# Second part's q from a natural-order table, three list segments, pinned scatters and later lists in a sparse attention kernel

## The chip, the cores and the metric

The kernel runs on one core of a Trainium2 chip. The engines named here are PE (TensorE, matrix products, with its weight loads shown as PEld), DVE (VectorE), ACT (ScalarE), POOL (GpSimd, which here mostly issues indirect DMAs) and SP (SyncE, which issues plain DMAs). The metric is the device time of one execution in microseconds (us). Three runs of the kernel before took 1813.91, 1814.09 and 1817.4 us, a median of 1814.09.

## The reference

One graph attention layer over N = 4096 nodes with D = 512 features and H = 8 heads of 64, all in float32. The adjacency matrix is 4096 x 4096 int32 and sparse: a node has about 17 neighbours, itself among them.

```python
hs = layer_norm(x, ln1_scale, ln1_bias)
ht = layer_norm(h_target, ln1_scale, ln1_bias)
q = (ht @ Wq + bq).reshape(T, H, HD) / sqrt(HD)
k = (hs @ Wk + bk).reshape(S, H, HD)
v = (hs @ Wv + bv).reshape(S, H, HD)
logits = einsum('thd,shd->hts', q, k)
logits = where(adj != 0, logits, -1e30)
ctx = einsum('hts,shd->thd', softmax(logits), v).reshape(T, D)
ht = layer_norm(ht + ctx @ Wo + bo, ln2_scale, ln2_bias)
y = ht + gelu(ht @ W1) @ W2
out = layernorm(x + y)
```

## The kernel before

**Lists instead of a dense matrix.** The kernel builds, for every node (a row), the list of its neighbours, and then works only on these. A row of adjacency is read in four quarters of 1024 columns. ACT turns a quarter into bytes of 0 and 1 (L729), DVE reads two bytes as one 16-bit word, multiplies it by a number that grows with the position (L734, `lio`), and takes the eight largest words of each of SQ = 5 segments of a quarter (L736). From these 20 x 8 words it splits the low and the high byte (L743, L744), adds the offset of the segment (L748, L751), and picks the 24 largest of 320 numbers in three rounds (L755, L757). All 320 numbers of a row also go to DRAM (`rest_d`, L767) for the few rows with more neighbours. A check that the counts agree guards this. If it fails, a slow general path runs.

**Two parts, sorted.** Rows 0 to 2047 are the first part and rows 2048 to 4095 the second. Within a part, `sort` (L808) ranks the rows by their number of neighbours on DVE and PE, and 16 indirect DMAs of POOL (L854) scatter the records of the rows (count, row number, normalisation, list) into rank order in DRAM. 128 rows of like length make a tile, and a tile is worked through with as many slots as its longest row needs: 302 slots for the first 16 tiles (tile 0 to 15, with 11 slots at first, up to 39) and 301 for tiles 16 to 31.

**Stages.** First the projections: for each block of 256 rows of x, normalise, transpose, make k and v, and write them to a DRAM table `kvd` (L936). Beside them the lists of the first part, and of the first five blocks of the second, are made. Then attention runs tile by tile over all 32 tiles. `prefetch` (L971) loads a tile's record with a DMA of POOL's queue (L980). `front` (L983) makes q: it gathers the tile's rows of h_target (POOL), scales them (L999, ACT), transposes them (L1003, PE), applies the first layer norm's scale and bias (L1006, ACT), multiplies by Wq (L1012, PE), and scales and adds the bias (L1017, DVE). The normalised rows stay transposed in the other half of `tq`. For each slot of the tile, POOL gathers 128 rows of 4 KB from `kvd` into a ring of buffers (L1076 calls the gather, which the profile shows at L967). Three slots make a step: DVE multiplies k by q (L1220) and sums over each head (L1225), ACT takes the exponential, DVE multiplies v of two slots by it (L1184) and ACT that of the third (`by_scalar`, L1204), and PE sums the slots by transposing them into PSUM (L1192). In the second part DVE first adds two slots (L1188), which saves PE a third of that. `finish` (L1078) masks, normalises, transposes the residual back by PE (L1112), multiplies by Wo (L1116), copies the sum out (L1121, ACT), and normalises again. `feed` (L1310) is the feed-forward of a group of one or two tiles (L1325 and L1334 on PE).

**What sets the order.** The program is written as generators, each of which yields a virtual cost. `_weave` (L400) always continues the one with the least virtual time. Attention and feed-forward take 60 units for a group of two tiles. `other_lists`, the remaining 11 blocks of lists and then `sort(1)`, starts at WAIT = 40 units and takes 18 units for a block. When the program is built, each engine's instructions are put in a fixed order from this program order and from when they should be ready. `tc.issue_after(ins)` puts what is written inside it behind `ins` on that engine. Every engine then runs its instructions in that order, and an instruction that waits holds up those behind it. Buffers have names and a number of copies (`bufs`): `xt`, `gt`, `h2T`, and `t` and `pf` in PSUM have two each, and a third user waits until one is free.

## Time and profile before

| | |
|---|---|
| median of three runs | 1814.09 us |
| profiled execution | 1817.49 us |
| its span, first to last instruction | 1815.5 us |
| mean granted clock of TensorE | 0.967 |
| busy: PE, DVE, ACT, POOL | 1677.8, 1436.5, 1224.1, 982.2 us |
| share of the span | 92%, 79%, 67%, 54% |
| DMA | 463.26 MB, mean 255 GB/s |
| gathers of kvd rows | 603, of 1257 ns each on POOL |

The profile is of one execution. A row of groups gives line, engine, operation, output and inputs with their shapes and the number of instructions, then busy time and mean ns of one, and at the end the idle time of the engine just before them with what ended it. A slice table gives the busy share of each engine in tenths over 40 equal slices. A wait row says which instruction waited for which, with the total, the number of times and the longest. A busy PE is not PE at its peak, since matmuls are pipelined and their ends are modelled, and POOL's times don't include the time to issue. A float32 product of 512 columns is two instructions in the trace.

### The profile page before, as it was taken

What the parts mean: (1) busy time and instruction counts of PE and PEld (TensorE: products, weight loads), DVE (VectorE), ACT (ScalarE), POOL (GpSimd) and SP (SyncE); (2) the same over time, 40 slices, a digit from 0 to 9 for tenths busy, and PEclk for the clock granted to TensorE, in tenths of its full rate; (3) what the DMA queues carried; (4) which work ended last, traced back from release to release, by engine and by line L of the source; (5) the groups of instructions that cost most, each with busy time, mean ns of one, the idle gap of its engine ahead of it and who ended that gap; (6) DMA issues with size and microseconds to landing.
All of it is one profiled execution on the core that took longest, in us unless ns stands there. A gap on an engine that the chain in (4) does not pass through costs nothing. (4 is left out here: it accounts for less than half of the span.)

```text
span 1815.5 us, 22973 instructions
## 1 busy us (share of the span) xinstructions
PE 1677.8 (92%) x7030; PEld 1097.9 (60%) x7030; DVE 1436.5 (79%) x2660; ACT 1224.1 (67%) x3121; POOL 982.2 (54%) x834
## 2 busy tenths in 40 slices
PE   7989984597999979999999989999999999999997
PEld 3434442465766656766776757666666666666664
DVE  6989876899999837777978989978878797988200
ACT  5767654487987736766778868877777676787311
POOL 1000144656566676766678788867575665763101
PEclk9999996698999989999999999999999999999998
DMA  9999968989887557777878878787776776774000
GB/s 344 366 380 372 344 198 319 404 287 332 271 305 256 201 173 243 258 255 267 273 263 302 293 260 295 249 285 250 241 266 222 248 251 238 244 248 153 18 6 26
DMA packets 140269, 463.26 MB, mean 255 GB/s; under 512 B 16500, under 2 KB 21672, under 8 KB 140136
## 3 DMA queue, kind: packets, MB, share of 16 engines
q0 software_dynamic: 96656, 342.64, 55.8%
q1 hardware_dynamic: 35664, 95.98, 15.0%
q10 hardware_dynamic: 7816, 23.08, 3.3%
q8 instruction: 58, 0.95, 0.2%
q14 instruction: 75, 0.61, 0.1%
HBM read 430.75 MB, written 30.89 MB: 254 GB/s over the span
## 5 line engine op out<-in xcount | busy, mean ns | idle before, releaser
L967 POOL DMA_INDIRECT kv<-kvd,rec x603 | 758.1, 1257 | 347.5 <-PE cps L1192 139.7
L1334 PE MATMUL po<-w,gt 128*128 128x512 f32 x1024 | 466.4, 598 | 16.2 <-ACT gt L1328 16.2
L1325 PE MATMUL pf<-h2T,w 128*128 128x256 f32 (+1 forms) x2176 | 465.9, 368 | 0.1
L1325 PEld LDWEIGHTS pf<-h2T,w 128*128 128x128 f32 x2176 | 389.3, 191 | 64.5 <-issue 20.3
L1220 DVE TENSOR_TENSOR kv<-kv,tq 128x1536 f32<-128x1536 f32 (+2 forms) x211 | 351.6, 1675 | 68.3 <-DMA kv<-kvd,rec 56.2
L1204 ACT ACTIVATE kv<-kv,pa 128x64 f32<-128x64 f32 x1520 | 391.0, 336 | 4.3
L1225 DVE TENSOR_REDUCE lg<-kv 128x24 f32<-128x1536 f32 (+2 forms) x211 | 350.1, 1666 | 1.4
L1334 PEld LDWEIGHTS po<-w,gt 128*128 128x128 f32 x1024 | 188.8, 192 | 212.4 <-issue 194.3
L1192 PEld LDWEIGHTS cps<-ident,kv 128*128 128x128 f32 x2008 | 240.2, 145 | 109.4 <-issue 59.2
L1192 PE MATMUL cps<-ident,kv 128*128 128x128 f32 x2008 | 264.5, 280 | 44.1 <-DVE kv L1184 24.5
L1184 DVE TENSOR_TENSOR kv<-kv,p 128x1024 f32<-128x1024 f32 (+1 forms) x211 | 251.0, 1193 | 22.8 <-ACT p L1229 20.3
L687 POOL TENSOR_TENSOR n_rs<-n_ve,mhalf 128x2 f32<-128x2 f32 (+2 forms) x51 | 50.8, 997 | 329.1 <-DVE n_ve L680 165.3
L729 ACT ACTIVATE kv<-kv 128x1024 uint8<-128x1024 int32 x128 | 134.9, 1056 | 100.0 <-DMA kv<-in_adj_dram 51.7
L1328 ACT ACTIVATE gt<-pf 128x512 f32<-128x512 f32 x128 | 76.4, 597 | 93.8 <-PE pf L1325 75.8
L1328 ACT ACT_TABLE_LOAD x104 | 133.4, 1283 | 1.7
L736 DVE MAX8 cand<-kv 128x8 uint16<-128x103 uint16 (+1 forms) x640 | 131.8, 252 | 0.8 <-DVE R L755 0.2
L930 PE MATMUL pq<-wk,h2T 128*128 128x512 f32 x256 | 120.8, 616 | 12.1 <-ACT tq L932 7.2
L1012 PE MATMUL t<-wq,tq 128*128 128x512 f32 x256 | 118.2, 605 | 5.6 <-ACT tq L1006 5.6
L930 PE MATMUL pq<-wv,h2T 128*128 128x512 f32 x256 | 115.5, 594 | 6.4 <-ACT kv L729 3.0
L1229 ACT ACTIVATE p<-lg 128x24 f32<-128x24 f32 (+2 forms) x179 | 39.2, 219 | 113.0 <-DVE lg L1225 88.8
L1116 PE MATMUL t<-wo,rb 128*128 128x512 f32 x256 | 115.2, 592 | 0.0
L930 PEld LDWEIGHTS pq<-wk,h2T 128*128 128x128 f32 x256 | 48.9, 197 | 69.9 <-issue 55.2
(160 smaller groups left out, 1582.2 us busy)
## 6 DMA issues: line engine op xcount, KB each, us to landing
kv<-in_adj_dram SPq DMA_DIRECT2D x128, 512.0 KB
kvd<-tq ACTq DMA_DIRECT2D x24, 512.0 KB
kv<-kvd,rec POOLq DMA_INDIRECT x603
kv<-in_L_gnn_h_target_dram SPq DMA_DIRECT2D x32, 256.0 KB
kv<-in_x_dram SPq DMA_DIRECT2D x15, 512.0 KB
rest_d<-gid SPq DMA_DIRECT2D x32, 160.0 KB
w<-in_L_gnn_W_dram SPq DMA_DIRECT2D x4, 1024.0 KB
kvd<-kv ACTq DMA_DIRECT2D x8, 512.0 KB
```

Source lines behind the costliest of these rows:

```text
L729: nc.scalar.activation(sg, a, AF.Sign, accum_out=dpart[:, i, h:h + 1])
L736: nc.vector.max(cand[:, h * SQ + s, :], wd[:, w0:w1])
L930: nc.tensor.matmul(pkv, hT[:, kc, j * P:(j + 1) * P], w[:, kc, :], start=kc == 0, stop=kc == KC - 1)
L967: nc.gpsimd.indirect_dma_start(out=dst, out_offset=None, in_=table[:, :], in_offset=bass.IndirectOffsetOnAxis(ap=idx, axis=0))
L1184: nc.vector.tensor_tensor(v4, v4, p[:, j0:j0 + m, :].unsqueeze(3) .to_broadcast([P, m, H, HD]), ALU.mult)
L1192: nc.tensor.matmul(cps[:, c, :], kv[:, j, D + c * P:D + (c + 1) * P], ident, is_transpose=True, start=j0 + j == 0 and c == 0, stop=j0 + n ...
L1204: newest[:] = [nc.scalar.mul(v, v, pa[:, hd:hd + 1]).ins]
L1220: nc.vector.tensor_tensor(kv[:, :n, :D], kv[:, :n, :D], tq[:, :D].unsqueeze(1).to_broadcast([P, n, D]), ALU.mult)
L1225: nc.vector.tensor_reduce(lg[:, :n, :], kv[:, :n, :D].rearrange("p j (h d) -> p j h d", h=H), AX.X, ALU.add)
L1325: nc.tensor.matmul(pf[:, k, :], w1[(f0 + k) // KC][:, kc, (f0 + k) % KC * P:((f0 + k) % KC + 1) * P], h2T[:, kc, :w], start=kc == 0, stop= ...
L1328: nc.scalar.activation(gt, pf, AF.Gelu_apprx_tanh)
L1334: nc.tensor.matmul(po[j], gt[:, k, j * P:(j + 1) * P], w2[(f0 + k) // KC][:, (f0 + k) % KC, :], start=False, stop=f0 + k == FC - 1, skip_g ...
```

## The change

There are five edits.

1. A new generator, `natural`, makes q of the second part's 16 blocks of rows in natural order and writes a table `qd` in DRAM with a row of 4 KB for each node: q, and beside it the normalised row with its bias, not transposed. It is woven in with 5 units a block, from virtual time 0 on. `front` of a tile of the second part then only gathers its rows of `qd`. `finish` of such a tile leaves out the transposes of the residual, and DVE adds it in place of the copy by ACT.
2. SQ goes from 5 to 3. A segment then has up to 171 words. The position numbers grow by 1 in place of 2, so that they still fit a byte, and the sum of offset and number is made with a factor of 2 in place of the plain addition.
3. For tiles 0 to 2 (LEAN = 3) the third slot is multiplied by DVE with the other two, and `by_scalar` isn't called.
4. The scatters of the records are put behind the gather issued last, in program order (`behind(issues)`). The record of a tile of the second part is loaded by SP's queue in place of POOL's. The copy of its tags is put behind the last sum of logits.
5. WAIT goes from 40 to 80: `other_lists` starts later.

```diff
@@ -1,4 +1,4 @@
-from contextlib import ExitStack
+from contextlib import ExitStack, nullcontext
 
 import concourse.bass as bass
 import concourse.tile as tile
@@ -488,7 +488,7 @@
     NQ = 4
     QW = N // NQ
     WQ = QW // 2
-    SQ = 5
+    SQ = 3
     WS = -(-WQ // SQ)
     SEGS = [(s * WS, min(s * WS + WS, WQ)) for s in range(SQ)]
     SEG = NQ * SQ
@@ -512,6 +512,7 @@
     kvd = dram.tile([N + P, 2 * D], F32, name="kvd")
     recs_d = [dram.tile([n * P, RW], I32, name=f"rec{i}") for i, (_, n) in enumerate(PARTS)]
 
+    qd = dram.tile([NBT * P, 2 * D], F32, name="qd")
     rest_d = dram.tile([N, 2 * SEG * 8], F32, name="rest_d")
 
     flag = const.tile([1, 1], I32, name="flag")
@@ -608,12 +609,12 @@
 
             def list_constants():
                 io = turn_of("wide", wide)
-                nc.gpsimd.iota(io[:, :SQ * WS], pattern=[[0, SQ], [2, WS]], base=1,
+                nc.gpsimd.iota(io[:, :SQ * WS], pattern=[[0, SQ], [1, WS]], base=1,
                                channel_multiplier=0)
 
                 nc.vector.tensor_copy(lio, io[:, :WQ])
                 io = turn_of("wide", wide)
-                nc.gpsimd.iota(io[:, :2 * SEG], pattern=[[1, 2], [QW, NQ], [2 * WS, SQ]], base=0,
+                nc.gpsimd.iota(io[:, :2 * SEG], pattern=[[1, 2], [QW, NQ], [2 * WS, SQ]], base=-1,
                                channel_multiplier=0)
                 nc.gpsimd.iota(io[:, 2 * SEG:2 * SEG + NB], pattern=[[1, NB]], base=0,
                                channel_multiplier=0)
@@ -713,6 +714,9 @@
                     a = turn_of("wide", wide)
                 nc.sync.dma_start(a, adj[i * P:(i + 1) * P, h * QW:(h + 1) * QW])
                 return a
+
+            def behind(ins):
+                return tc.issue_after(ins[-1]) if ins else nullcontext()
 
             def edges(i):
 
@@ -748,7 +752,7 @@
                 nc.vector.scalar_tensor_tensor(gid, dec, 0.0,
                                                off.unsqueeze(2).to_broadcast([P, 2 * SEG, 8]),
                                                op0=ALU.is_gt, op1=ALU.mult)
-                nc.vector.tensor_add(gid, gid, dec)
+                nc.vector.scalar_tensor_tensor(gid, dec, 2.0, gid, op0=ALU.mult, op1=ALU.add)
                 flat = gid.rearrange("p s e -> p (s e)")
                 for r in range(RE // 8):
                     top = rec[:, E0 + r * 8:E0 + (r + 1) * 8]
@@ -851,10 +855,11 @@
                 nc.vector.tensor_copy(ranki, rank)
                 yield 10.0
                 for i in range(n):
-                    ins = nc.gpsimd.indirect_dma_start(
-                        out=recs_d[part][:, :],
-                        out_offset=bass.IndirectOffsetOnAxis(ap=ranki[:, i:i + 1], axis=0),
-                        in_=R[:, i, :], in_offset=None)
+                    with behind(issues):
+                        ins = nc.gpsimd.indirect_dma_start(
+                            out=recs_d[part][:, :],
+                            out_offset=bass.IndirectOffsetOnAxis(ap=ranki[:, i:i + 1], axis=0),
+                            in_=R[:, i, :], in_offset=None)
 
                     tc.declare_no_dep(ins.ins, group=f"scatter{part}", reason="other rows")
                     tc.add_to_no_dep_group(f"scatter{part}", ins.ins)
@@ -962,11 +967,12 @@
 
 
             recs, tqs, h2Ts, done, ready, latest, newest = {}, {}, {}, set(), [], [], []
+            issues, logits = [], []
 
             def gather(dst, table, idx):
-                nc.gpsimd.indirect_dma_start(
+                issues[:] = [nc.gpsimd.indirect_dma_start(
                     out=dst, out_offset=None, in_=table[:, :],
-                    in_offset=bass.IndirectOffsetOnAxis(ap=idx, axis=0))
+                    in_offset=bass.IndirectOffsetOnAxis(ap=idx, axis=0)).ins]
 
             def prefetch(i):
                 if i >= NT or i in recs:
@@ -977,7 +983,7 @@
                 r0 -= PARTS[part][0] * P
                 rec = sp.tile([P, E0 + MAXE], I32, name="rec", bufs=6)
 
-                nc.gpsimd.dma_start(rec[:, :RW], recs_d[part][r0:r0 + P, :])
+                (nc.sync if part else nc.gpsimd).dma_start(rec[:, :RW], recs_d[part][r0:r0 + P, :])
                 recs[i] = rec
 
             def front(i, idle=0):
@@ -985,6 +991,14 @@
 
                 rec = recs[i]
                 tq = sp.tile([P, 2 * D], F32, name="tq", bufs=3)
+                if TILES[i][0] >= PARTS[1][0] * P:
+                    gather(tq, qd, rec[:, ROW:ROW + 1])
+                    for _ in range(3 + idle):
+                        yield
+                    with behind(logits):
+                        nc.vector.tensor_copy(tags[:, i, :], rec[:, DEG:TGT + 1])
+                    tqs[i] = tq
+                    return
                 t = tq[:, :D]
                 gather(t, h_target, rec[:, TGT:TGT + 1])
                 for _ in range(1 + idle):
@@ -1108,17 +1122,22 @@
                 yield
                 pa = ps.tile([P, D], F32, name="t", bufs=2)
 
+                natural_q = TILES[i][0] >= PARTS[1][0] * P
+                if not natural_q:
+                    for c in range(KC):
+                        nc.tensor.matmul(pa[:, c * P:(c + 1) * P], tq[:, D + c * P:D + (c + 1) * P],
+                                         ident, is_transpose=True, start=c == 0, stop=False,
+                                         skip_group_check=True)
                 for c in range(KC):
-                    nc.tensor.matmul(pa[:, c * P:(c + 1) * P], tq[:, D + c * P:D + (c + 1) * P],
-                                     ident, is_transpose=True, start=c == 0, stop=False,
-                                     skip_group_check=True)
-                for c in range(KC):
-                    nc.tensor.matmul(pa, ct[:, c, :], wo[:, c, :], start=False,
+                    nc.tensor.matmul(pa, ct[:, c, :], wo[:, c, :], start=natural_q and c == 0,
                                      stop=c == KC - 1, skip_group_check=True)
                 turned.add(i)
                 yield
                 h = sp.tile([P, D], F32, name="h")
-                nc.scalar.copy(h, pa)
+                if natural_q:
+                    nc.vector.tensor_add(h, pa, tq[:, D:])
+                else:
+                    nc.scalar.copy(h, pa)
                 yield
                 stats(sp, h, mv[:, len(hs), :], "n2")
                 hs.append(h)
@@ -1179,7 +1198,7 @@
 
 
 
-                    m = n - 1 if n == S else n
+                    m = n - 1 if n == S and i >= LEAN else n
                     v4 = kv[:, :m, D:].rearrange("p j (h d) -> p j h d", h=H)
                     nc.vector.tensor_tensor(v4, v4, p[:, j0:j0 + m, :].unsqueeze(3)
                                             .to_broadcast([P, m, H, HD]), ALU.mult)
@@ -1222,9 +1241,9 @@
                                                     ALU.mult)
                             lg = sp.tile([P, S, H], F32, name="lg")
                             latest[:] = [lg[:, 0, 0:1]]
-                            nc.vector.tensor_reduce(lg[:, :n, :],
-                                                    kv[:, :n, :D].rearrange("p j (h d) -> p j h d", h=H),
-                                                    AX.X, ALU.add)
+                            logits[:] = [nc.vector.tensor_reduce(
+                                lg[:, :n, :], kv[:, :n, :D].rearrange("p j (h d) -> p j h d", h=H),
+                                AX.X, ALU.add).ins]
                             if j0 > 0:
                                 nc.scalar.activation(p[:, j0:j0 + n, :], lg[:, :n, :], AF.Exp)
                             advance()
@@ -1236,7 +1255,7 @@
                             if j0 == 0:
                                 p = sp.tile([P, MAXE, H], F32, name="p", bufs=1)
                                 nc.scalar.activation(p[:, :n, :], lg[:, :n, :], AF.Exp)
-                            if n == S:
+                            if n == S and i >= LEAN:
                                 by_scalar(kv, lg)
                             last = j0 + n == TILES[i][1]
                             after = finish(i, p, cps, group, hs, mv) if last else None
@@ -1373,11 +1392,66 @@
                                                    op0=ALU.bypass, op1=ALU.max)
 
 
+            def natural():
+
+                Rf = Rs[1].bitcast(F32)
+                ht, hTs = {}, {}
+
+                def load(b):
+                    if b < NBT:
+                        ht[b] = sp.tile([P, D], F32, name="xt")
+                        r0 = (PARTS[1][0] + b) * P
+                        nc.sync.dma_start(ht[b], h_target[r0:r0 + P, :])
+
+                def norm(b):
+                    if b < NBT:
+                        nc.scalar.activation(ht[b], ht[b], AF.Identity,
+                                             bias=Rf[:, b, RST + 1:RST + 2],
+                                             scale=Rf[:, b, RST:RST + 1])
+
+                def turn(b):
+                    t = ht.pop(b)
+                    pt = ps.tile([P, KC, P], F32, name="t", bufs=2)
+                    for kc in range(KC):
+                        nc.tensor.transpose(pt[:, kc, :], t[:, kc * P:(kc + 1) * P], ident)
+                    hT = sp.tile([P, KC, P], F32, name="gt")
+                    for kc in range(KC):
+                        nc.scalar.activation(hT[:, kc, :], pt[:, kc, :], AF.Identity,
+                                             bias=b1r[:, kc:kc + 1], scale=s1c[:, kc:kc + 1])
+                    hTs[b] = hT
+
+                def make(b):
+                    hT = hTs.pop(b)
+                    pq = psf.tile([P, D], F32, name="pf")
+                    for kc in range(KC):
+                        nc.tensor.matmul(pq, hT[:, kc, :], wq[:, kc, :], start=kc == 0,
+                                         stop=kc == KC - 1)
+                    pb = psf.tile([P, D], F32, name="pf")
+                    for kc in range(KC):
+                        nc.tensor.transpose(pb[:, kc * P:(kc + 1) * P], hT[:, kc, :], ident)
+                    qn = sp.tile([P, 2 * D], F32, name="h2T")
+                    nc.vector.scalar_tensor_tensor(qn[:, :D], pq, HD ** -0.5, bqr,
+                                                   op0=ALU.mult, op1=ALU.add)
+                    nc.scalar.copy(qn[:, D:], pb)
+                    nc.sync.dma_start(qd[b * P:(b + 1) * P, :], qn)
+
+                load(0)
+                load(1)
+                norm(0)
+                for b in range(NBT):
+                    turn(b)
+                    load(b + 2)
+                    norm(b + 1)
+                    yield 2.5
+                    make(b)
+                    yield 2.5
+
             def chain(gens):
                 for g in gens:
                     yield from g
 
-            WAIT = 40.0
+            WAIT = 80.0
+            LEAN = 3
             AHEAD = 4
             UNIT = 60.0
 
@@ -1448,7 +1522,7 @@
                 yield from sort(1)
 
             _weave((att, 0), (chain(feed(g) for g in range(len(GROUPS))), 0), (other_lists(), WAIT),
-                   (weights(), 0))
+                   (natural(), 0), (weights(), 0))
 
     left = nc.values_load(flag[0:1, 0:1], min_val=0, max_val=1)
     with tc.If(left != 0):
```

## The prediction

> **What bounds the kernel now.** The chain that ended last covers only the final 3 us, so it says nothing. I read the slices of the page first, to see the stages (a slice is 45.4 us).
>
> ```profile
> PE   7989984597999979999999989999999999999997
> DVE  6989876899999837777978989978878797988200
> PEclk9999996698999989999999999999999999999998
> DMA  9999968989887557777878878787776776774000
> ```
>
> PE is full almost everywhere. It isn't in slices 7 and 8, where the projections end and attention begins: the clock is low there too, and DMA is full. DVE has one hole, at slice 15. Next, stages, cut at the starts of the last list-edge masking of each tile (L1083: tile 2 ends at 387, tile 7 at 585, tile 8 at 631, tile 9 at 695, tile 15 at 1013, tile 31 at 1681). After the clock times come PE, PE's weight loads, DVE, ACT, POOL, then granted clock and DMA.
>
> ```profile
> 0.00:296.00 296.00, 255.46 (x675) 118.59 (x676) 246.20 (x1060) 190.68 (x354) 44.47 (x62) 0.97 0.92 330
> 296.00:387.00 91.00, 54.54 (x266) 40.48 (x265) 76.09 (x105) 48.82 (x153) 63.12 (x52) 0.74 0.95 358
> 387.00:631.00 244.00, 231.47 (x1076) 160.94 (x1075) 233.49 (x487) 194.31 (x495) 144.07 (x120) 0.97 0.81 280
> 631.00:695.00 64.00, 54.05 (x242) 37.42 (x241) 32.89 (x33) 32.73 (x89) 46.92 (x42) 0.92 0.57 197
> 695.00:1013.00 318.00, 308.83 (x1445) 216.32 (x1444) 255.40 (x263) 231.61 (x644) 226.53 (x185) 0.99 0.79 265
> 1013.00:1681.00 668.00, 651.87 (x2818) 442.60 (x2817) 579.94 (x644) 500.64 (x1348) 445.82 (x362) 0.99 0.74 248
> 1681.00:1816.00 135.00, 121.56 (x515) 81.59 (x513) 12.53 (x73) 25.33 (x46) 11.29 (x13) 0.96 0.05 17
> ```
>
> So PE bounds 695 to the end (97 to 98%), PE and DVE together bound 387 to 631 (95 and 96%), and 296 to 387 is a start with PE idle for 36.5 us of 91 and running at 0.74 of its clock. The second part (tiles 16 to 31) is the 668 us stage. Its groups on PE that make q:
>
> ```profile
> L1012 PE MATMUL t<-wq,tq 128*128 128x512 f32 x122 | 55.4, 596 | 4.9 <-ACT tq L1006 4.9
> L1112 PE MATMUL t<-ident,tq 128*128 128x128 f32 x60 | 9.0, 273 | 0.0
> L1003 PE MATMUL t<-ident,tq 128*128 128x128 f32 x60 | 9.0, 272 | 0.0
> ```
>
> and the waits of that stage which belong to q and to the ring:
>
> ```profile
> POOL kv L967 <- PE cps L1192: 54.0, 36, 8.4
> ...
> DVE tq L1017 <- PE t L1012: 24.2, 5, 6.2
> ```
>
> Last, the hole at 631, in order of time on POOL and DVE. Nine scatters of the second part's records run back to back from 627; gathers behind them come late, and DVE waits 9.4 us for one.
>
> ```profile
> 627.06 1.01 POOL L854 DMA_INDIRECT rec<-R,kv  x1 [1.53 <-DVE kv L851]
> ...
> 638.89 0.96 POOL L854 DMA_INDIRECT rec<-R,kv  x1 [0.30 <-issue]
> 640.16 0.97 POOL L967 DMA_INDIRECT kv<-kvd,rec  x1 [0.30 <-issue]
> ```
> ```profile
> 664.35 1.76 DVE L1220 TENSOR_TENSOR kv<-kv,tq 128x1536 f32<-128x1536 f32 x1 [9.37 <-DMA kv<-kvd,rec]
> ```
>
> **What the Trainium skill says.** "TensorE: Matmul & The Clock Gate", Part 1: an idle PE falls to half its clock and needs sustained work to get it back. The trace agrees: clock 0.62 between 310 and 360. "DMA: Bandwidth & Descriptors", Issuing engines are not separate DMA queues: transfers of all issuers share 16 engines. It agrees: 405 GB/s at share 1.03 in those 50 us, with gathers, weights and adjacency together. "VectorE: DVE Perf Modes", Mode 1×: one element a cycle at 0.96 GHz. MAX8 agrees: (478 - 253) ns over (320 - 103) elements is 1.04 ns each. "ScalarE: Activation LUTs", Table sets: copy and identity are in every set, so the new scalings need no table load; the group L1006 (Identity) indeed shows none.
>
> **The change, part by part.** The sum is against the profiled execution: 1817.5 us, of which 1815.5 are the span; it is 3.4 over the median 1814.1, and I subtract from the median at the end.
>
> 1. *q of the second part moved to the start (natural).* Removed from each of its tiles: PE 73.4 us over 15 tiles (the three rows above), 4.9 each; ACT 0.81 + 4 x 0.37 + 0.57 (L999, L1006, L1121) = 2.9; DVE 0.68 (L1017) + 0.22 (L995), while the residual add costs 0.68 (like L1104), so DVE is about even. Added to virtual time 0 to 80, which is tiles 0 to 2, the 296 to 387 stage: 16 x (4 transposes 0.60, 8 matmuls 3.60, 4 transposes 0.60 = 4.8, as those rows run in order of time) = 77 us of PE; ACT 16 x 2.9 = 46; DVE 16 x 0.68 = 11; SP 16 loads and 16 stores. Bytes: 16 x (0.25 read + 0.5 written) = 12 MB, at 405 GB/s 30 us of transfer, put beside gathers of 0.5 MB each; what the lists no longer load there, about 3 MB, comes off. PE's spare in that stage is 36.5 idle plus about 13 of the 54.5 busy (clock 0.74 with full-rate work after 370): 49. So 77 - 49 = 28 us of extra length; transfers alone would ask for (12 - 3)/0.405 = 22 less the 4 that the share leaves free, so they agree. Bounds: +10 (q work starts before 296, in the 25 us that PE idles from 260 to 296) and +110 (the clogged rival below).
> 2. *Second-part stage with 73 us less PE.* PE 652 - 73 = 579. But DVE keeps 577, and POOL 446 plus about 0.3 us of issue for each of 362 instructions = 555, less 16 record loads of 0.6 + 0.3 that go to SP's queue, 541. SP issues nothing else there, so these cost nothing; if SP were held up, a tile's record would be late, and POOL's gathers with it. A gather of q is 512 KB for 256: 4 MB over 600 us, hidden under a DMA share of 0.74. If PE stayed at 97.6% the stage would be 593 (-75). Two engines as closely loaded as DVE and PE now become stood at 95 to 96% from 387 to 631; with a third near I take 94%: 579/0.94 = 616, that is -52. Bounds -75 and -15. DVE's 24 us behind L1017 vanish in it; DVE next waits for POOL's power or for the ring.
> 3. *Three segments.* Five MAX8 in a row take 0.93, 0.186 each; three of 171 words take 3 x (0.186 + 68 x 1.04 ns) = 0.77: -0.16 x 4. Seven operations on 192 in place of 320 columns: -0.133 x 7. Together -1.6 us of DVE a tile; by group means -2.1. Before 296, 21 tiles: -33 to -44, but PE (255 of 296) and DMA bound that stage. Its tail, 247 to 290, has PE waiting for copies that stand behind Sign activations on ACT, which wait for adjacency and sign buffers (5 or 6 of ACT's waits, 15 + 7 us). I take -6, bounds -15 and 0.
> 4. *Lists later (WAIT 80).* About nine us of lists leave the start (DVE 76 + 11 - 9 there) and fall into 387 to 631, where DVE is at 96%: 10.5 tiles at 7.8 for 7.75 at 9.4 is +9 of DVE. I take +8, bounds 0 and +15. The records are asked for at virtual 405; the scatters now end at 346 in place of 306, so they are still 60 units, some 65 us, early.
> 5. *Scatters pinned.* Each of the 16 (1.27 us of POOL) goes behind the gather last issued, one in 3 units, so no nine in a row. The tile that took 64.3 us should take what its neighbours take, 45 to 48, plus some: -14, bounds -18 and 0. What waits behind a scatter now is one gather, not nine scatters' worth.
> 6. *Third slot by VectorE in tiles 0 to 2.* 11 full segments: DVE +11 x (1.75 - 1.21) = +6, ACT -11 x 2.2 = -24. Hidden both ways (DVE 84 of 119, ACT 49 + 46 - 24 = 71 of 119). Without that cover it costs DVE's 6.
>
> Sum: +28 - 52 - 6 + 8 - 14 = -36; 1817.5 - 36 = 1781.5, and 1778 by the median.
>
> **Rivals.** *A, PE was not what bound the second part.* POOL's 86 us behind the ring (54 for cps, 33 for L1188) and DVE's 87% stay; the stage gives back 15 to 25 instead of 52. For it: three engines would all be above 90%. Against: DVE and PE ran at 96 and 95% together before. Time: -36 + 35 = -1 to -10, so 1804 to 1813; centre 1807. *B, slower: natural clogs the start.* It shares two buffers each of xt, gt, h2T, t and pf with attention and the feed-forward. If a tile of it runs as one chain (load, 0.8, 0.6, 1.5, 3.6, 0.7, write, with load and write under a full DMA some 5 us together), 12 us each and 16 x 12 = 192 us from 290, attention's PE and ACT instructions stand behind it in order and tile 2 ends at 482: +95 in place of +28, so -36 + 67 = +31, 1845. It decides from 28 + 36 = +64: tile 2 ending after 451, about 10 us a tile. For it: DMA is full just there. Against: the loads run two ahead, and PE needs 4.8. *C, no faster lists or a lost list:* in the reference's inputs no third of a quarter row holds more than eight words with an edge, so the fallback isn't taken; I give it nothing. *D, the scatters behind gathers that wait for the ring move the hole instead of filling it:* -14 falls away, 1792; it lies in the forecast's range.
>
> **How the numbers follow.** Forecast with D: 0.56, own range 1740 to 1800. A: 0.20. B: 0.20. Something not listed: 0.04. No change that a measurement of this kernel can tell from nothing is 0.2%, 3.6 us. A's upper end gives 0.05 to "same"; B and 0.02 more are slower, 0.22; the rest is faster, 0.73. The range takes in A and half of B: 1738 to 1838.
>
> **What would show it.** Step 1: between 296 and 420 PE full at clock near 1, tile 2 ending near 415. Step 2: the last sixteen tiles in about 616 us, PE and DVE both near 94%, no wait of DVE for q. Step 3: three MAX8 of about 324 ns a quarter row. Steps 4 and 5: scatters apart by 3 us or more, no tile near 64 us, DVE full until about tile 9. The prediction is wrong if tile 2 ends after 451 (B), or if the last sixteen tiles still take 645 us (A).

## The result, and the profile after

The changed kernel is slower. Its median is 1913.0 us (four runs, 1902.88 to 1914.93) beside 1814.38 for the kernel before on the same chip: a ratio of 1.0525, 95% interval 1.049 to 1.056. (The ratios are estimates from several runs of both kernels and need not equal the quotient of two medians, here 1.0543.) The forecast was 1778, range 1738 to 1838. The profiled execution is the shortest of the four, 1902.88 us with a span of 1901.2 us, so the stages below account for 85 us over the profiled execution before, of the 99 between the medians.

The slices of the changed kernel's page (47.5 us each):

```profile
PE   7999977888798989998999998989899988989995
DVE  6898755687887667767697898989798877768200
PEclk9999989899898999999999999989899999999998
DMA  9999889877875757567787897888888776674000
```

Slices 7 and 8 of PE, a 4 and a 5 before, are a 7 and an 8, and its clock is up in them, as forecast. But DVE, which stood at 9 in slices 9 to 13 of before, is at 6 to 8 from slice 9 to 20, and PE is less often at 9 in the second half.

The stages, cut at the same tile ends as before (the masking, L1083 before, is L1097 now: tile 2 ends at 420, tile 8 at 708, tile 9 at 761, tile 15 at 1098, tile 31 at 1762; what follows tile 31 is called the tail). After the times come PE, PE's weight loads, DVE, ACT, POOL, the granted clock, and DMA's share and rate:

```profile
0.00:296.00 296.00, 262.94 (x693) 122.40 (x693) 221.23 (x876) 192.59 (x359) 50.74 (x70) 0.97 0.94 341
296.00:420.00 124.00, 100.78 (x387) 57.04 (x388) 90.08 (x127) 59.60 (x137) 47.94 (x40) 0.89 0.86 316
420.00:708.00 288.00, 255.59 (x1168) 175.39 (x1167) 221.42 (x402) 188.83 (x492) 138.34 (x121) 0.93 0.70 239
708.00:761.00 53.00, 50.82 (x240) 36.03 (x239) 36.94 (x39) 35.59 (x98) 30.50 (x28) 1.00 0.69 238
761.00:1098.00 337.00, 318.46 (x1486) 221.35 (x1485) 260.19 (x268) 231.48 (x639) 239.07 (x199) 0.99 0.75 254
1098.00:1762.00 664.00, 608.40 (x2577) 418.36 (x2575) 567.85 (x623) 470.73 (x1260) 447.02 (x349) 0.95 0.75 253
1762.00:1901.00 139.00, 117.42 (x489) 77.78 (x487) 14.17 (x76) 24.91 (x45) 11.29 (x13) 0.94 0.05 16
```

Stage by stage, before to after: 296 to tile 2's end 91 to 124 (+33), tiles 3 to 8 244 to 288 (+44), tile 9 64 to 53 (-11), tiles 10 to 15 318 to 337 (+19), the last sixteen tiles 668 to 664 (-4), the tail 135 to 139 (+4). Two things stand out. Up to the end of tile 2 the loss is about as forecast (the end was expected near 415 and came at 420), but tiles 3 to 8 then lose another 44 us, where 8 were forecast. And the last sixteen tiles have 43 us less of busy PE and are almost as long as before. What the waits of these sixteen tiles say, first a row of DVE in the kernel before, then DVE's and POOL's in the changed one:

```profile
DVE kv L1220 <- DMA kv<-kvd,rec: 3.8, 2, 2.0
```
```profile
DVE kv L1239 <- DMA kv<-kvd,rec: 64.2, 21, 7.4
...
DVE n_nm L693 <- POOL n_rs L688: 27.5, 4, 10.4
```
```profile
POOL kv L973 <- DVE kv L1207: 52.7, 19, 8.1
...
POOL kv L973 <- PE cps L1211: 12.0, 25, 2.2
```

PE hardly holds the ring of gather buffers any more (12.0 us in place of 54.0), DVE's wait for q is gone, and yet DVE waits 64.2 us for gathers, which took 3.8 before. The wait has moved: POOL's gathers now wait most for DVE's addition (L1207), and DVE for the gathers.

### The profile page after: what moved, and what is told of

The parts are those of the page before. It is cut to its first block, busy times and chain, and to the rows that moved or that the text cites. A ratio compares the mean times of both kernels' runs of the same rounds, so it can differ in the third digit from the quotient of the medians.

```text
span 1901.2 us, 22747 instructions
## 1 busy us (share of the span) xinstructions
PE 1714.4 (90%) x7030; PEld 1108.3 (58%) x7030; DVE 1411.9 (74%) x2404; ACT 1203.7 (63%) x3022; POOL 964.9 (51%) x818
## 5 line engine op out<-in xcount | busy, mean ns | idle before, releaser
L973 POOL DMA_INDIRECT kv<-kvd,rec x603 | 743.7, 1233 | 408.2 <-PE cps L1211 177.1
L1353 PE MATMUL po<-w,gt 128*128 128x512 f32 x1024 | 478.0, 610 | 15.9 <-ACT gt L1347 15.8
L1344 PE MATMUL pf<-h2T,w 128*128 128x256 f32 (+1 forms) x2176 | 472.8, 371 | 0.0
L1344 PEld LDWEIGHTS pf<-h2T,w 128*128 128x128 f32 x2176 | 393.3, 193 | 65.7 <-issue 20.4
L1223 ACT ACTIVATE kv<-kv,pa 128x64 f32<-128x64 f32 x1432 | 368.4, 336 | 4.4
L1211 PEld LDWEIGHTS cps<-ident,kv 128*128 128x128 f32 x2008 | 235.3, 142 | 85.7 <-issue 42.7
L1211 PE MATMUL cps<-ident,kv 128*128 128x128 f32 x2008 | 260.6, 276 | 19.6 <-DVE kv L1207 16.1
L1203 DVE TENSOR_TENSOR kv<-kv,p 128x1024 f32<-128x1024 f32 (+2 forms) x211 | 256.7, 1222 | 18.8 <-ACT p L1248 18.7
L740 DVE MAX8 cand<-kv 128x8 uint16<-128x171 uint16 (+1 forms) x384 | 111.7, 325 | 1.1
L935 PEld LDWEIGHTS pq<-wk,h2T 128*128 128x128 f32 x256 | 48.9, 197 | 64.9 <-issue 49.5
```

The source lines that it names most:

```text
L935: nc.tensor.matmul(pkv, hT[:, kc, j * P:(j + 1) * P], w[:, kc, :], start=kc == 0, stop=kc == KC - 1)
L973: issues[:] = [nc.gpsimd.indirect_dma_start(out=dst, out_offset=None, in_=table[:, :], in_offset=bass.IndirectOffsetOnAxis(ap=idx, axis=0) ...
L1203: nc.vector.tensor_tensor(v4, v4, p[:, j0:j0 + m, :].unsqueeze(3) .to_broadcast([P, m, H, HD]), ALU.mult)
L1211: nc.tensor.matmul(cps[:, c, :], kv[:, j, D + c * P:D + (c + 1) * P], ident, is_transpose=True, start=j0 + j == 0 and c == 0, stop=j0 + n ...
L1223: newest[:] = [nc.scalar.mul(v, v, pa[:, hd:hd + 1]).ins]
L1344: nc.tensor.matmul(pf[:, k, :], w1[(f0 + k) // KC][:, kc, (f0 + k) % KC * P:((f0 + k) % KC + 1) * P], h2T[:, kc, :w], start=kc == 0, stop= ...
```

## The experiments

**Halves of the change, and single edits.** First q in natural order alone (edit 1), then all but it, then two small edits by themselves: three segments, and the pinned scatters with the record loads of the second part on SP.

```diff
# q alone, set against the changed kernel
-    SQ = 3
+    SQ = 5
-            WAIT = 80.0
-            LEAN = 3
+            WAIT = 40.0
+            LEAN = 0
# and scatters not pinned, records loaded by POOL's queue
# (the copy of the tags stays behind the last sum of logits)
# all but q: the changed kernel with
-                   (natural(), 0), (weights(), 0))
+                   (weights(), 0))
# and front and finish as in the kernel before
```

> Only edit 1 (q of the second part made early and gathered), with five segments, third slot by ACT in all tiles, scatters free, records on POOL's queue, lists from 40. If the early q is the cause, most of the 99 us are here: 1880 to 1915, with the tiles 1 to 3 taking about 150 us together (78 before, 154 in the changed kernel) and the last sixteen tiles 650 to 668. If the cause is the pins or the late lists, this kernel is at 1770 to 1825.

> Edits 2 to 5 without the early q: three segments, third slot by VectorE in tiles 0 to 2, pinned scatters and record loads on SP, lists from 80. If the early q is the cause, this is as fast as before or faster: 1785 to 1820, with no tile of 64 us at the scatters. If the pins or the late lists are the cause, 1870 or more, and the sixteen tiles of the second part at 664 with 73 us more of PE work would become about 700.

> Only edit 2, three segments in place of five. By the sum of the prediction DVE has 1.6 us less in each of 32 blocks of lists: -6 us before attention and up to -17 where DVE bounds: 1790 to 1808. A theory that only a new order of the instructions costs time has no size for it: then it may also lie above 1818.

> Only the pinned scatters and the second part's record loads on SP's queue. By the prediction's sum -14: 1796 to 1810, the tile at the scatters 45 to 50 us in place of 64. If pinned scatters hold up the gathers behind them, the tiles 8 to 11 take longer together than the 200 us of before and the time is 1820 or more.

Measured against 1812.53 us for the kernel before: q alone 1881.3 (ratio 1.0381, 1.0343 to 1.0418), all but q 1853.88 (1.0232, 1.0206 to 1.0258), segments alone 1822.06 (1.0059, 1.0034 to 1.0085), pins with record loads 1822.32 (1.0047, 1.0022 to 1.0072). So q costs 69 us, and the rest 41; the sum is 110 where the whole change costs 99. Q alone came as expected in total, though tiles 1 to 3 took 128 us and not about 150. All but q fell between its two expectations, and segments and pins each came out slower, where a gain was expected. No single edit that was tried brings anything.

With three segments the eight-largest search is as short as forecast (327 and 323 ns in the changed kernel, where 324 was worked out) and tile 0 ends 10 us earlier, at 333. But tiles 6 to 8 take 144 us in place of 125, and tile 9 ends at 702, 7 later than before. The lists had become cheaper, and that was no time on the path. What exactly shifts in tiles 6 to 8 I didn't separate. The two profiled executions, 1819.53 and 1817.49, are also only 2 us apart, so these stages show a part of the 10 between the medians.

**Does the second part gain, and what does natural cost?** The next kernel takes q's work out of the second part without putting it anywhere. Set against q alone:

```diff
-                    gather(tq, qd, rec[:, ROW:ROW + 1])
+                    gather(tq, h_target.rearrange('(n k) d -> n (k d)', k=2), rec[:, ROW:ROW + 1])
...
-                   (natural(), 0), (weights(), 0))
+                   (weights(), 0))
```

> The kernel with q alone in natural order, less natural itself: a tile of the second part gathers its rows of 4 KB from h_target seen as rows of 1024, in place of the table of q. It leaves out layer norm and product that make q of the second part; the exponentials take the scale 1/8. Nothing is added at the start, so tile 2 should end at 387 like before, and what is left is what the second part gains from 73 us less of PE. Theory now (the second part is bound by the loop of VectorE, gather and ring as soon as PE has room): last sixteen tiles 645 to 658 us in place of 668, total 1790 to 1804. Rival (the step as forecast, PE bound): last sixteen tiles 605 to 630, total 1752 to 1778; then natural at the start would also slow the second part.

It took 1802.1 us (0.9912, 0.9883 to 0.9941, of 1817.79 before). Tile 15 ends at 1018, as good as before's 1013, and the last sixteen tiles take 651 us in place of 668. So even with nothing put elsewhere, q's removal gains 17 us in the second part, not 52. Q alone has 652 there, so natural doesn't disturb the second part; but its tile 15 ends at 1096, 78 us later. That is the price of natural by the profiled executions: 78 us in the first part for 17 in the second.

Why 78? The groups of natural in the kernel with q alone, between 296 and 563:

```profile
L1427 PE MATMUL pf<-wq,gt 128*128 128x512 f32 x128 | 68.2, 681 | 6.0 <-ACT gt L1419 5.5 <-ACT h2T L1435 0.3
...
L1416 PE MATMUL t<-ident,xt 128*128 128x128 f32 x64 | 11.1, 292 | 13.5 <-DVE tq L1031 7.0 <-ACT h L1140 4.8 <-ACT xt L1408 1.1
...
L1431 PE MATMUL pf<-ident,gt 128*128 128x128 f32 x64 | 9.7, 273 | 2.1 <-ACT gt L1347 2.1
```

They add up to 89 us, 5.6 a block. That is more than they add to PE's busy time, since rows of groups overlap: PE is busy 417 us from 296 to the end of tile 9 with q alone, 340 before and 337 without q's work, so natural adds 77 to 80. Either this PE time is the price, or the chain around it (load, copies, two shared `h2T` buffers, a write that lands after 9.0 us in the changed kernel). Two kernels tell these apart. One leaves three of the four products of a block out; the other gives natural four times as long, 20 units a block.

```diff
# a quarter of the product
-                    for kc in range(KC):
-                        nc.tensor.matmul(pq, hT[:, kc, :], wq[:, kc, :], start=kc == 0,
-                                         stop=kc == KC - 1)
+                    nc.tensor.matmul(pq, hT[:, 0, :], wq[:, 0, :], start=True, stop=True)
# spread
-                    yield 2.5
+                    yield 10.0
```

> The kernel with q alone in natural order, with one of the four products that make a block's q (it leaves out three quarters of q's sum in the second part; loads, transposes, copies, buffers and the write of 512 KB stay). That takes 6 of 8 matmul instructions a block out, some 16 x 6 x 0.53 = 51 us of PE by the group's busy time in that kernel. Theory (natural costs its PE time, and none of PE's idle time at the start takes it in): the first sixteen tiles end 40 to 52 us earlier, 1045 to 1056 in place of 1096, and the total is 1829 to 1842. Rival (natural's own chain of load, copies, write and shared buffers costs, whatever PE does in it): tile 15 ends at 1080 to 1096, total 1866 to 1882.

> The kernel with q alone in natural order, with natural given 20 units a block in place of 5: four times as long, over tiles 0 to 10. Theory (the burst is what costs: shared buffers and in-order engines in a start that has little room): tile 3 ends at 430 to 445 in place of 482, each block costs its 4.8 us of PE where PE is full, and the total is 1840 to 1862. Rival (work of natural costs more than its PE time wherever it stands, by the waits that it puts in front of attention): 1875 to 1900.

The quarter product took 1845.68 us (1.0167, 1.0146 to 1.0189) and its tile 15 ends at 1059, 37 us earlier. Both figures are 3 or 4 us above the range of the theory and far from that of its rival. Stages from 296 to the end of tile 9, first of the kernel before, then of q alone, then with a quarter of the product:

```profile
296.00:695.00 399.00, 340.06 (x1582) 238.84 (x1581) 342.47 (x623) 275.87 (x735) 254.11 (x212) 0.91 0.81 285
```
```profile
296.00:774.00 478.00, 417.42 (x1831) 275.56 (x1830) 355.59 (x634) 304.51 (x818) 241.44 (x212) 0.93 0.74 262
```
```profile
296.00:736.00 440.00, 375.23 (x1734) 256.45 (x1733) 352.58 (x632) 303.94 (x817) 247.97 (x212) 0.92 0.80 285
```

The stage is PE's busy time and a remainder that stays: 399 - 340 = 59, 478 - 417 = 61, 440 - 375 = 65. PE's busy time falls by 42 and the stage by 38. So natural costs its PE time at nearly the full price, and PE's idle time in this stretch takes none of it in, taken as a whole. The chain around it costs little beside that.

The remainder is the same in size but not in place. With q alone, up to the end of tile 2, in tiles 3 to 8 and in tile 9:

```profile
296.00:424.00 128.00, 101.92 (x385) 57.64 (x384) 87.01 (x138) 77.09 (x226) 51.71 (x47) 0.89 0.90 332
424.00:710.00 286.00, 261.01 (x1206) 180.24 (x1205) 235.07 (x463) 194.02 (x503) 141.71 (x125) 0.95 0.71 245
710.00:774.00 64.00, 54.48 (x243) 37.69 (x242) 33.50 (x35) 33.40 (x92) 48.01 (x42) 0.92 0.58 194
```

Up to tile 2 PE now idles 26 us where it idled 36.5, so some 10 were filled, as the forecast meant. But in tiles 3 to 8 it idles 25 where it idled 12.5. ACT's waits for adjacency between 296 and the end of tile 10, with WAIT still at 40, grow beside that from 12.1 us to 34.1, so natural delays the late lists too; that this is what opens the new holes isn't shown. Why the sum stays so nearly the same is open; it may be chance.

Spread over four times as long, natural costs the same: 1888.52 us (1.0395, 1.0363 to 1.0427), tile 3 ends at 430 and not at 482, but tile 15 at 1096 once more. That is the rival's figure of time, though not its reason: the work has to be done somewhere, and neither placing found room for it. From 296 to the end of tile 15 PE idles 70 us with q alone and 75 with natural spread, beside 68 before and 71 without q's work.

A kernel that was to put natural's rows into three ring slots instead of `h2T` told nothing of buffers: two of those slots also take the adjacency of the late lists (`wide`, L568) and the third their bytes. Lists were overwritten, by this reading of the program, and the slow general path ran, which the trace shows.

> The kernel with q alone in natural order, with the rows on their way to DRAM held in three ring slots that the first part leaves unused, in place of the two h2T buffers. Theory (write of 9 us and two shared buffers set 8.4 us a block and hold up the feed-forward): a block takes 5 to 6 us, tile 3 ends at 445 to 460 in place of 482, total 1850 to 1865. Rival (PE, PSUM buffers and the order on PE and ACT set the pace): tile 3 ends at 470 to 485, total within 8 us of 1881.

It took 7821.49 us.

**What sets the pace of the second part.** Starting from the kernel without q's work (651 us in that stage), I took something else away each time: the two powers that go from DVE to POOL and back, DVE's addition of two slots, half of the feed-forward's second product, and one step of the gathers' lead.

```diff
# no power
-                nc.gpsimd.tensor_tensor(rs, ve, mhalf[:, :n], ALU.pow)
+                (nc.vector.tensor_copy(rs, ve) if name in ('n2', 'n3') else
+                 nc.gpsimd.tensor_tensor(rs, ve, mhalf[:, :n], ALU.pow))
# no addition
-                        nc.vector.tensor_add(kv[:, 0, D:], kv[:, 0, D:], kv[:, 1, D:])
# half of the output product
-                        for k in range(fb):
+                        for k in range(1, fb, 2):
# one step less ahead
-                ahead = AHEAD + (1 if k >= first_b else 0)
+                ahead = AHEAD
```

> The kernel without q's work in the second part, with the power of the second and third normalisation (VectorE to GpSimd and back) left out: VectorE copies the variance in its place. In that kernel VectorE was busy for 566 us of the second part's 651, waited 49.5 for gathers and 22.9 for the power, and the power's instructions stand among the gathers in GpSimd's order. Theory (the loop of VectorE and gathers, in order on GpSimd, bounds the second part once PE has room): the last sixteen tiles take 620 to 638 us. Rival (PE's own order and the chains behind it still set the pace): 645 to 655.

> The kernel without q's work in the second part, with VectorE's addition of two slots left out (the second slot of a step is then missing from the sum; PE transposes as many slots as with the addition). VectorE had 566 us of work in the last sixteen tiles' 651, of which the addition is 69; PE had 599. Theory (VectorE's length in the loop with the gathers sets the pace): the last sixteen tiles take 605 to 625 us, with PE at 96% or more. Rival (gathers, in GpSimd's order and in the ring, or PE's order set it): 638 to 651.

> The kernel without q's work in the second part, with half of the feed-forward's second product left out in all tiles (every other block of 128 features is missing from its sum). PE had 599 us of work in the last sixteen tiles' 651, of which this product is 225, so PE falls to some 487. Theory (PE's length no longer counts there; the loop of gathers, ring and VectorE does): the last sixteen tiles take 630 to 650 us. Rival (PE still sets the pace through its order, at about 92% of its time): 575 to 605, where VectorE's 566 would be next.

> The kernel without q's work in the second part, with the gathers of a step asked for four steps ahead in the second part in place of five; work and buffers stay. Theory (the loop of gathers sets the pace): the last sixteen tiles take 660 to 690 us in place of 651, and VectorE's waits for gathers go from 49.5 to 65 or more. Rival (PE and VectorE in their own order set it, and gathers only show it): 645 to 656, with waits like before.

The stage in these kernels: without q's work, without the power, without the addition, and with half of the output product. All four lack q's work.

```profile
1018.00:1669.00 651.00, 599.33 (x2563) 410.81 (x2562) 566.40 (x622) 472.36 (x1262) 459.13 (x360) 0.97 0.77 258
```
```profile
1013.00:1653.00 640.00, 597.03 (x2568) 406.69 (x2567) 567.72 (x638) 469.45 (x1260) 437.96 (x345) 0.97 0.78 263
```
```profile
1020.00:1683.00 663.00, 600.26 (x2558) 412.65 (x2557) 514.16 (x522) 467.75 (x1257) 431.64 (x361) 0.95 0.75 255
```
```profile
976.00:1586.00 610.00, 520.62 (x2364) 379.72 (x2362) 565.26 (x625) 473.42 (x1264) 466.99 (x361) 0.91 0.82 277
```

- *Without the power* 640 us (total 1786.44; 0.9838, 0.9808 to 0.9867): 11 less. It lies between the two expectations. The trip to POOL is part of the path, but not most of what is missing.
- *Without the addition* 663 us (total 1818.58; 1.0000, 0.9986 to 1.0014), longer than with it, though DVE has 52 us less to do. Both expectations fell. DVE's wait for gathers grew from 49.5 to 109.8 us, about what was taken away, and PE, with the same 600 us of work, waited 39.5 us for the normalised rows in place of 15.7 (first the two rows without q's work, then without the addition too):

```profile
DVE kv L1242 <- DMA kv<-kvd,rec: 49.5, 22, 7.8
...
PE t L1162 <- ACT h L1153: 15.7, 7, 6.8
```
```profile
DVE kv L1241 <- DMA kv<-kvd,rec: 109.8, 44, 7.6
...
PE t L1162 <- ACT h L1153: 39.5, 13, 10.2
```

  So DVE's length alone is not the bound there. Why the stage even grew is open; the order that the program gets without these instructions is a guess.
- *One step less ahead* 650 us (total 1798.81; 0.9881, 0.9854 to 0.9909), DVE's wait for gathers 51.1 us. But the kernel hardly did what was meant. POOL's order changed in a few places only (a power stands three gathers earlier, for one), and the gathers run as early as before: the last gather of a step starts 15.6 us before DVE's product (median over tiles 17 to 30), where it was 15.2 us with the longer lead. So the theory of the gathers' lead is left untested, and so is the size of the ring, which no run changed.
- *Half of the output product* 610 us (total 1683.59; 0.9267, 0.9250 to 0.9284). PE's busy time falls by 79 and the stage by 41. Neither expectation holds: PE's length still counts, at half its price. DVE now has no wait for gathers among its rows, and one large wait:

```profile
DVE n_nm L693 <- POOL n_rs L688: 41.2, 6, 10.0
```

  565 us of work and 41 of this wait are 606 of the 610. By this reading DVE, with its trip to POOL, is the bound here; no kernel took that trip out as well.

Taken together: from 652 to 599 us of PE the stage gives back 17 of 53, from 599 to 521 41 of 79. Between a stage that PE fills (97.6%) and one that DVE fills lies a wide stretch in which a microsecond of PE was worth a third to a half. That the two hold each other up by turns there, in the fixed orders of their programs, fits these runs but isn't shown. That the waits for gathers are where this shows, and not its cause, is supported by the kernel without the addition alone. No single wait was found whose removal restores the 35 us between 616 and 651.

**The lists that start later.** WAIT alone, at 80, 60 and 20, in the kernel before:

```diff
-            WAIT = 40.0
+            WAIT = 80.0
```

> The kernel before with WAIT = 80 in place of 40, and nothing else. The runs so far put segments alone at +10 and pins alone at +9, and all edits but q at +41, so if the parts add up, later lists and the third slot on VectorE together have +22 left. Theory: the later lists are what costs, because the Sign activations of ACT then wait for adjacency loads in the middle of full attention, with the exponentials behind them in order: +15 to +25 (1828 to 1838), with tiles 6 to 8 above 50 us each, and tile 9 still near 64. Rival: the price is that of the third slot or of an interplay of edits: within 6 us of before, 1808 to 1820.

> The kernel before with WAIT = 60 in place of 40, and nothing else. Theory (a straight line): 1830 to 1840. Rival (a collision that begins at some point): within 6 us of before or already at 1850 to 1860.

> The kernel before with WAIT = 20 in place of 40, and nothing else. WAIT = 80 cost 41 us, 1.0 us a unit. Theory (every list that moves out of the start goes where VectorE and ACT are full, so the price is a straight line): 1790 to 1804. Rival (a collision that begins past 40): 1810 to 1822, or slower, since DMA is at 92% between 296 and 387 already.

| WAIT | total us | ratio to before | ACT waits for adjacency, 296 to the end of tile 10 |
|---|---|---|---|
| 20 | 1829.45 | 1.0069 (1.0052 to 1.0085) | 7.6 us, 3 times |
| 40 (before) | 1817.5 and 1817.8 | 1 | 12.1 us, 4 times |
| 60 | 1836.92 | 1.0109 (1.0081 to 1.0138) | 33.0 us, 9 times |
| 80 | 1858.79 | 1.0227 (1.0188 to 1.0266) | 45.6 us, 13 times |

From 40 on these three points lie on a line, 1 us for each unit, and below 40 it turns back up: with 20 tile 8 takes 69 us (it ends at 654 where before has 631). So 40 was the best of these places. WAIT = 80 was expected to cost 15 to 25 us and to leave tile 9 near 64; it cost 41, and tile 9 took 54. The 41 us of all the edits but q are as much as WAIT's 41; segments, pins and the third slot together add nothing to them.

Most of the loss lies in tiles 3 to 8. In the kernel before with WAIT = 80 they take 283 us in place of 244:

```profile
380.00:663.00 283.00, 242.14 (x1081) 166.43 (x1081) 234.72 (x488) 188.53 (x488) 137.56 (x118) 0.90 0.71 244
```

DVE has 234.7 us of work there, where it had 233.5. So it isn't more work of DVE that makes these tiles longer; DVE idles 48 us in place of 10.5.

A stretch of ACT's work in order of time, of the same kernel. Start, duration, operation and, in brackets, the idle time before:

```profile
507.97 1.06 ACT L729 ACTIVATE kv<-kv 128x1024 uint8<-128x1024 int32 x1 [5.98 <-DMA kv<-in_adj_dram]
...
516.94 1.06 ACT L729 ACTIVATE kv<-kv 128x1024 uint8<-128x1024 int32 x1 [6.31 <-DMA kv<-in_adj_dram]
...
521.02 1.06 ACT L729 ACTIVATE kv<-kv 128x1024 uint8<-128x1024 int32 x1 [2.93 <-DMA kv<-in_adj_dram]
...
524.48 1.06 ACT L729 ACTIVATE kv<-kv 128x1024 uint8<-128x1024 int32 x1 [2.31 <-DMA kv<-in_adj_dram]
...
526.94 0.22 ACT L1238 ACTIVATE p<-lg 128x24 f32<-128x24 f32 x1
```

Four Sign activations of the lists wait 17.5 us in all for adjacency quarters, which come through two buffers, and the first exponential of a tile stands behind them. On DVE the lists' product waits for the Sign and attention's product stands behind it:

```profile
518.12 0.42 DVE L734 TENSOR_TENSOR kv<-kv,lio 128x512 uint16<-128x512 uint16 x1 [4.85 <-ACT kv L729]
...
518.47 3.42 DVE L1220 TENSOR_TENSOR kv<-kv,tq 128x1536 f32<-128x1536 f32 x2
521.80 3.41 DVE L1225 TENSOR_REDUCE lg<-kv 128x24 f32<-128x1536 f32 x2
```

The sums that the exponential needs begin only at 521.80, since DVE was held, so only the last Sign, at 524.48, can have held the exponential itself. The rest of the delay in this stretch went by way of DVE.

The Trainium skill says of these engines' queues ("PSUM — Partial Sum Buffer", Engine vs sequencer instructions) that they are strictly first in, first out, and here it can be watched: DVE's product, at 518.47, starts only behind the lists' product, which waited 4.85 us for the Sign. PE still has the feed-forward to do meanwhile; then it runs dry. The two stretches, from 502 and from 527 us (columns as in the stages):

```profile
502.00:527.00 25.00, 20.64 (x88) 13.61 (x86) 16.66 (x41) 7.46 (x13) 6.58 (x7) 0.98 0.90 316
527.00:545.00 18.00, 7.89 (x27) 5.63 (x28) 15.44 (x17) 17.78 (x49) 8.96 (x5) 0.50 0.40 125
```

This is the mechanism that the waits show. That ACT's wait grows with WAIT by 33.5 us where the time grows by 41 speaks for it, but no kernel took that wait away with WAIT left at 80. Nor does the size of the wait by itself give the time: it is 33.0 us with WAIT = 60, which costs 19, and 34.3 us with all edits but q, which cost 41.

Last, the changed kernel with WAIT at 40 again, to see how the two costs stand together.

```diff
-            WAIT = 80.0
+            WAIT = 40.0
```

> The changed kernel with WAIT back at 40, and nothing else. WAIT = 80 alone cost 41 us, q alone 69, and the two sum to 110 where the change cost 99. Theory (the two costs are separate, later lists in tiles 4 to 10 and natural's work in tiles 2 to 6): 1866 to 1882. Rival (lists and natural collide when both begin early, which WAIT = 80 was there to avoid): 1900 or more.

It took 1882.18 us (1.0367, 1.0346 to 1.0389): the same as q alone. WAIT = 80 thus costs 31 us in the changed kernel by the medians. By the two profiled executions, 1892.0 and 1902.88, it is only 11, and these lie in the last sixteen tiles (653 and 664 us), with tile 15 at 1094 and 1098. So by the profiles the first part doesn't pay twice. ACT's waits for adjacency up to the end of tile 10 fit that, 36.2 us with WAIT at 40 and 32.2 with 80, but what makes natural and late lists overlap isn't shown. Why the second part is 11 longer, tile 29 above all (38.9 and 54.1 us), is open.

**The scatters alone.** Pinned behind the last gather, the record loads left on POOL:

```diff
-                for i in range(n):
-                    ins = nc.gpsimd.indirect_dma_start(
+                for i in range(n):
+                    with behind(issues):
+                        ins = nc.gpsimd.indirect_dma_start(
```

> The kernel before with its scatters pinned behind the gather issued last, and nothing else: the record loads of the second part stay on GpSimd's queue. Pins with record loads on SyncE's queue were +9, with tile 9 at 57.4 and tile 10 at 60.9 us, and a tail that was 9 longer. Theory (the scatters only move their delay to the next tile, so pinning gains nothing, and what was lost came with the record loads): 1808 to 1818. Rival (pinning itself costs): 1819 to 1828.

1817.29 us (1.0012, 1.0001 to 1.0022). Tile 9 falls from 64.3 to 58.7 us and tile 10 rises from 47.9 to 59.6. The hole moves, it doesn't fill: tile 11 ends at 785 in both kernels. With the record loads on SP's queue it was 1822.32, most of it in a tail of 144 us in place of 135; why loads that end earlier lengthen the tail I can't say.

## Why the prediction was wrong

Three terms of the sum carry most of the miss: step 1 was off by 50 us, step 2 by 35 and step 4 by 33.

*Step 1, natural at the start: +28 forecast, +78 measured. The step failed at PE's spare time, "36.5 idle plus about 13", which was taken off as 49 us.* PE's work was forecast rightly: 77 us, and PE's busy time grew by 77 to 80. But its idle time was counted as room, 36.5 us up to the end of tile 2, and another 13 for a faster clock. Up to there some 10 were filled, and about as many came back in tiles 3 to 8, so that the idle time up to the end of tile 9 stays at 59 to 65 us whatever is added. What keeps it there, attention's own chain of waits or the lists that natural delays, isn't separated. The 13 didn't come either: PE's instructions other than natural's took 338 us up to the end of tile 9, where without natural they took 337 to 340. The bounds, +10 to +110, held the result. Rival B had the right sign for the wrong reason: tile 2 ended at 420, well short of its point of decision at 451, and most of the loss came after it.

*Step 2, the last sixteen tiles: -52 forecast, -17 measured (-4 in the whole change). It failed at "I take 94%", and at "652 - 73".* PE's busy time fell by 53 and not by 73: the rows of groups overlap (PE's ten rows of before add up to 703.6 us where it was busy 651.9). Without q's three rows PE was busy for 593 of the 652, so only 59 were theirs alone, and what remained then took 599, at a clock of 0.97. And PE came to stand at 92%, with DVE at 87%, where I had taken 94% from another stage. This is rival A by its number, 15 to 25 for the stage, and its point of decision, 645 us, was passed. By its reason it is only in part: PE's length still counted, at a third to a half.

*Step 3, three segments: -6 forecast, +10 alone. It failed where the gain at the start was taken for the whole.* The operations' times were right. The gain at the start is there, and is lost in tiles 6 to 8.

*Step 4, later lists: +8 forecast, +41 alone. It failed at "+9 of DVE".* The sign and the stage were right, the term mis-sized five times. It was worked out as DVE's load, but DVE's work in tiles 3 to 8 grew by 1 us, and its idle time by 38. What was left out is what stands behind a Sign that waits, though ACT's waits for adjacency were among the waits read for step 3.

*Step 5, pinned scatters: -14 forecast, +2 alone by the ratio, and with the record loads +9. It failed at "no nine in a row".* Rival D. A delay of POOL's was counted as gone because it was cut in pieces.

*Step 6, third slot:* not tried alone. Beside q, three segments, pins and third slot together make no difference (1882.18 and 1881.3).

With the measured terms, +78 - 17 for q and 0 for what came to nothing beside it, the sum is +61; the medians say 69 for q alone, and 99 with WAIT, of which the stages explain only a part.

Three readings in the working were also wrong, without deciding anything. PE doesn't fill the tail: it is busy 121.6 of 135 us there, 90%. Between 260 and 296 it idles 18 us and not 25. And the stage's 15 to 25 in rival A make 1805 to 1815.

## What to carry to other kernels

Idle time of an engine with a fixed order is not room for more work until an experiment shows it. Here adding 77 us of PE work to a stretch in which PE idled 59 lengthened it by 79. A saving on the bounding engine need not be worth its size: here 53 us less of PE shortened a stage by 17. So take work out without putting it elsewhere, as the kernel without q's work does, before building the table that moves it. And what is started later must be followed on every engine that it waits on, with what stands behind it.

## What was not expected of the hardware

The mean time of a group can hide two speeds. Natural's product of 128 x 512 columns took 681 ns on average in the kernel with q alone, where such a product had taken 596 in the second part before. But its median is 592, and the longer ones lie mostly near 1061 ns. Two blocks of eight, and the two stretches that they lie in:

```profile
307.57 5.48 PE L1427 MATMUL pf<-wq,gt 128*128 128x512 f32 x8
...
319.89 3.60 PE L1427 MATMUL pf<-wq,gt 128*128 128x512 f32 x8
```
```profile
305.00:311.00 6.00, 4.33 (x9) 2.27 (x10) 6.00 (x7) 2.70 (x12) 4.78 (x5) 0.50 1.03 416
312.00:330.00 18.00, 16.97 (x70) 9.59 (x69) 14.97 (x24) 9.25 (x26) 10.50 (x9) 1.00 1.03 412
```

The first block began at a granted clock of 0.50 and took 5.5 us, the second ran at 1.00 and took 3.6. So a time taken from a full stage undervalues work that is moved into one where the clock drops. How full PE is doesn't settle it: the feed-forward's second product took 612 ns without q's work, with PE busy 92% of the stage, and 599 with half of it left out, with PE busy 85%.
